# A two-layer graph network on one core: layer 1's weighted sums computed with features on partitions and turned back

## The chip, the cores and the metric

The kernel runs on one core of one Trainium2 chip. The metric is device time in microseconds (us) of one execution, the median of several runs. TensorE (PE) multiplies matrices, VectorE (DVE), ScalarE (ACT) and GpSimd (POOL) work elementwise, and SyncE (SP) issues DMA transfers. Each engine works through its own instructions in program order; between engines only semaphores order the work.

## The reference

There are 16 graphs of 1024 nodes with 256 features each, in float32. Cut to what matters (`_layernorm`, weights and `SCALE` are as one expects):

```python
# layer 0: attention with 8 heads of 32 features over the neighbours
h = jnp.maximum(_layernorm(x), 0.0)
Q, K, V = proj(Wq, bq), proj(Wk, bk), proj(Wv, bv)
scores = jnp.where(adj[:, None] == 0, -inf, einsum('bhnd,bhmd->bhnm', Q, K) * SCALE)
out = einsum('bhnm,bhmd->bhnd', softmax(scores), V)
x = x + einsum('bno,po->bnp', merge_heads(out), Wo) + bo
# layer 1: scores between nodes, a softmax, and a weighted sum of h
h = jnp.maximum(_layernorm(x), 0.0)
e_k = leaky_relu(einsum('bid,bjd->bij', h * a_k[:, 0], h), 0.2)   # k = 0..3
scores = -9e15;  scores = e_k where adj == k + 1
x = x + einsum('bij,bjd->bid', softmax(scores), h)                # <- the sums
```

adj holds only 0 and 1 here, so the kernel computes layer 1 with a_0 alone and has a branch for other kinds that is not taken.

## The kernel before, in words

A tile is 128 nodes (rows) of one graph, so there are 16 x 8 = 128 tiles (`NT` = 8 per graph). One long pipeline runs over steps `s` = 0 to 128; `t` is `s` modulo 8. In one step the kernel does, side by side: attention of tile `s` (`now`), the end of attention of tile `s` - 1 (`was`), layer 1's scores and softmax of tile `s` - 9 (`edge`), the weighted sums and the output of tile `s` - 10 (`edge_was`), and the projections of tiles 8 and 9 ahead (`piece_was`, `piece`). After the last step a short loop over `tiles` (lines 987 to 1012) finishes the last nine layer-1 tiles; it is called the tail below.

The order of work is written by hand (`tc.manual_schedule()`): the order of the code is the order of the instructions on each engine. A step is a loop over eight heads `h`, and each `h` has a fixed order: `now.scores(h)` on PE (line 461, one tile of 128x1024 scores in PSUM), `now.softmax_max(h)` on DVE (line 473, adds the mask and takes the row's maximum), `softmax_exp` of the head before on ACT (line 490), then the turning of the head before that, either by PE transposes (line 590) and a copy (line 591) or by DVE's block transposition (`blocks_of`, line 381) and DMAs (`placed`, line 386), and then the extra work of that `h`. For the tile with t = 7 heads 4 and 5 are turned by PE, for t = 0 heads 0 and 1; for all others heads 0, 1, 4 and 5 go by blocks.

Scores are in two PSUM tiles, `sides`. Once layer 1 runs, heads 4 and 6 use `sides[1]` and all others `sides[0]`, so that scores(1), for example, can't start before softmax_max(0) has read `sides[0]`. Layer 1's scores (line 633, and transposes of mirrored blocks in line 627) use `sides[1]` in h = 0 to 2.

The other small results on PSUM live in two banks of 2 x 256 columns: `sums_place` and `brief` in the first, `early` and `late` in the second:

```python
sums_place, brief, early, late = (banks[i // 2][:, i % 2, :] for i in range(4))
```

What bears on the change, in a step's order. h = 4: `output` (PE, line 541, into `late`), `raised(1)` (ACT, line 309, reads `early`). h = 5: `residual` (DVE, line 547, reads `late`), layer-norm statistics (DVE), `gather(0)` (PE, line 698), `piece.turn` (PE, two transposes, line 237, into `late`), `turned` (ACT, lines 249 and 250). h = 6: scores(6), `gather(1)`, softmax_max(6), `store` (DVE, lines 705 and 707, and the output's DMA on SP, line 708), blocks of head 4, `project(0, ...)` (PE, line 267, eight instructions, into `late`). h = 7: scores(7), softmax_max(7), blocks of head 5, `combine(0)` (PE, line 526, writes `sums_place`), `raised(0)` (ACT, line 309, reads `late`).

`gather` computes the sums for one layer-1 tile. The transposed weights `pT` have 128 source nodes on partitions; `h1s` holds the normed features. For each of the eight blocks `j` of source nodes and each group `a` of 32 target nodes a matmul takes 32 columns of `pT` as the stationary operand and all 256 features as the moving one; its output goes to 32 partitions, so that four matmuls (`a` = 0 to 3) sit in four column groups of the array. A float32 matmul is two instructions in the trace; so there are 32 matmuls or 64 instructions for a tile. Target nodes are on partitions in the result, as the output wants them.

In the tail two PSUM places alternate for the sums: `sums_place` for even tiles, `late` for odd ones.

Of the kernel before, what the change touches and what calls it, by code (L numbers as in the profile page):

```python
# [14 lines left out]
ALU = mybir.AluOpType  # L15
AX = mybir.AxisListType

P = 128
HEADS = 8
HD = 32  # L20
# [22 lines left out]
def by_chunk(place):  # L43
    return place.rearrange("p (c n) -> p c n", n=P)
# [3 lines left out]
def gnn_kernel(  # L48
# [18 lines left out]
    nc = tc.nc  # L67
    B, N, D = x.shape
    NT = N // P
    NC = D // P  # L70
    SCALE = HD ** (-0.5)
    HALF = 512
    NB = P // HD
# [21 lines left out]
    sums_place, brief, early, late = (banks[i // 2][:, i % 2, :] for i in range(4))  # L95
# [5 lines left out]
    ident = const.tile([P, P], F32, name="ident")  # L101
# [269 lines left out]
    def mixed(rows):  # L371

        return rows.rearrange("(b k) n -> k b n", b=NB)
# [18 lines left out]
    h1s, x1ds, masks = {}, {}, {}  # L392
# [201 lines left out]
    class Edges:  # L594
# [98 lines left out]

        def gather(self, half):

            for j in range(half * NT // 2, (half + 1) * NT // 2):
                for a in range(NB):
                    nc.tensor.matmul(  # L698
                        self.sums[a * HD : (a + 1) * HD, :], lhsT=self.pT[:, j, a], rhs=h1s[self.b][:, j, :],
                        start=(j == 0), stop=(j == NT - 1),  # L700
                    )

        def store(self):
            rec = small.tile([P, 1], F32, tag="rec1")
            nc.vector.reciprocal(rec, self.total)
            ot = self.buffer("h0", [P, D])
            nc.vector.scalar_tensor_tensor(ot, self.sums, rec, self.x1, ALU.mult, ALU.add)  # L707
            nc.sync.dma_start(out=mixed(out[self.b, self.rows, :]), in_=ot)


    def layer_1_of_kinds(b):
# [75 lines left out]
    with tc.manual_schedule():  # L787
# [51 lines left out]
        for s in range(B * NT + 1):  # L839
            b, t = divmod(s, NT)  # L840

            def load_keys(h, end):
                if t == NT - 1 and b + 1 < B and 2 * h + end in KEY_STEPS:
                    load_key(b + 1, KEY_STEPS.index(2 * h + end))
                if t == 0 and 0 < b < B and 2 * (HEADS + h) + end in KEY_STEPS:
                    load_key(b, KEY_STEPS.index(2 * (HEADS + h) + end))

            nxt2, edge_nxt, piece_nxt = attend_of(s + 2), edges_of(s + 1), piece_of(s + 1)
            for h in range(HEADS):
                ending, eh = (now, h - 1) if h >= 1 else (was, HEADS - 1)  # L850
                turning, th = (now, h - 2) if h >= 2 else (was, HEADS + h - 2)

                load_keys(h, 0)


                if now:
                    now.scores(h)
                if h == 0 and piece_was:
                    piece_was.halve(0)
                if s == 0 and h == 1:  # L860
                    first[1].values()
                if h == 3 and edge:
                    edge.softmax_max()
                if h == 5:
                    if was:
                        was.residual()
                    norms(was, piece_nxt)
                if h == 6 and edge_was:
                    edge_was.gather(1)
                if now:  # L870
                    now.softmax_max(h)
                if h == 6 and edge_was:
                    edge_was.store()


                if h == 1 and edge:
                    edge.keep(0)
                if h == 2 and gone:
                    gone.turned_normed()
                if ending:  # L880
                    ending.softmax_exp(eh)

                if h == 3 and was:
                    was.turned_reciprocals()
                if h == 3 and edge:
                    edge.bend()
                    edge.keep(1)


                if h == 3:  # L890
                    if was:
                        was.combine(1)
                    if piece_was:
                        piece_was.biased()
                    if was:
                        was.combined()
                if turning and th in by_blocks(turning.t):
                    turning.turn_blocks(th)
                    turning.place_blocks(th)
                elif turning:  # L900
                    turning.turn(th, 0)
                    turning.turn(th, 1)


                if h == 0:
                    if edge:
                        edge.score(0)
                    if gone:
                        gone.normed()
                    if edge_was:  # L910
                        edge_was.turn_blocks()
                        edge_was.place_blocks()
                if h == 1:
                    if gone:
                        gone.turn_normed()
                    if piece_was:
                        piece_was.project(1, 0)
                        piece_was.project(1, 1)
                    if was:
                        was.reciprocals()  # L920
                    if piece_nxt:
                        piece_nxt.load()
                if h == 2:
                    if edge:
                        edge.score(1)
                    if piece_was:
                        piece_was.values()
                    if was:
                        was.turn_reciprocals()
                        was.add_bias()  # L930
                if h == 3:
                    if nxt:
                        nxt.load_queries()
                    if edge:
                        edge.leak()
                    if edge_was:
                        edge_was.load_nodes()
                    if nxt:
                        nxt.flag()
                        nxt.mask()  # L940
                if h == 4:
                    if was:
                        was.output()
                    if piece_was:
                        piece_was.raised(1)
                        piece_was.halve(1)
                    if piece:
                        piece.normed()
                    if piece_was:
                        piece_was.write_queries()  # L950
                    if edge_nxt:
                        edge_nxt.prepare()
                    if nxt2:
                        nxt2.load()
                if h == 5:
                    if edge_was:
                        edge_was.gather(0)
                    if piece:
                        piece.turn()
                    if piece:  # L960
                        piece.turned()
                if h == 6:
                    if edge:
                        edge.softmax_exp()
                    if was:
                        was.keep()
                    if now:
                        now.load_nodes()
                    if piece:
                        piece.project(0, 0)  # L970
                        piece.project(0, 1)
                if h == 7:
                    if now:
                        now.combine(0)
                    if piece:
                        piece.raised(0)
                load_keys(h, 1)
            gone, was, now, nxt = was, now, nxt, nxt2
            edge_was, edge = edge, edge_nxt
            piece_was, piece = piece, piece_nxt  # L980
# [7 lines left out]
        for i in range(1, len(tiles) + 2):  # L988
            edge = tiles[i] if i < len(tiles) else None
            if edge:  # L990
                edge.score(0)
                edge.score(1)
            if i <= len(tiles):
                tiles[i - 1].turn_blocks()
                tiles[i - 1].place_blocks()
            if i >= 3:
                tiles[i - 3].store()
            if i >= 2:
                tiles[i - 2].load_nodes()
            if edge:  # L1000
                edge.keep(0)
                edge.keep(1)
                edge.softmax_max()
                edge.bend()
                edge.leak()
                edge.softmax_exp()
            if i + 1 < len(tiles):
                tiles[i + 1].prepare()
            if i >= 2:
                tiles[i - 2].gather(0)  # L1010
                tiles[i - 2].gather(1)
        tiles[-1].store()


# [50 lines left out]
```

## Time and profile before

| | |
|---|---|
| median of 3 runs | 3076.24 us (3071.88 to 3076.31) |
| the profiled execution | 3076.4 us, of which the span from first to last instruction is 3074.5 us |
| mean granted TensorE clock | 0.996 |
| PE busy | 2965.6 us (96%) |
| ACT busy | 2654.5 us (86%) |
| DVE busy | 2515.6 us (82%) |
| POOL busy | 2177.6 us (71%) |

Busy time adds up the times at which at least one instruction of an engine is under way. PE's instructions overlap: a matmul of 128 columns lasts some 0.27 us in the trace, but the next one starts long before its end. What PE takes for something is therefore read from start to start in the timeline, not from the durations. In timeline lines, the first number is the start in us from the span's start, the second the time from the first start to the last end in the merged line, "x8" the number of instructions, and a bracket the idle time ahead and what ended it.

### The profile page before, as it was taken

The page shows a single profiled execution, that of the slowest core. Times are in us where ns is not written, and L with a number is a line of the kernel's source. Part 1 is how long each engine was busy: PE and PEld are TensorE (multiplying, and loading weights), DVE is VectorE, ACT ScalarE, POOL GpSimd, SP SyncE. Part 2 cuts the span into 40 slices and gives each one's busy share as a digit, 9 for nine tenths or more (in the row PEclk, how much of TensorE's full clock was granted, in tenths as well). Part 3 has the DMA queues.
Part 4 walks back from the last instruction along what each step waited for, and adds up shares of the span by engine and source line. Part 5 has one row for each costly group of instructions (what it writes and reads, how often), then busy time and mean ns, then how long its engine had stood idle before and what let it go on. Part 6 is the DMA issues. An engine that isn't in the chain of part 4 may idle for free. (4 is left out here: it accounts for less than half of the span.)

```text
span 3074.5 us, 96254 instructions
## 1 busy us (share of the span) xinstructions
PE 2965.6 (96%) x36722; PEld 2230.1 (73%) x36722; DVE 2515.6 (82%) x4453; ACT 2654.5 (86%) x5159; POOL 2177.6 (71%) x2999
## 2 busy tenths in 40 slices
PE   7889999999999999999999999999999999999998
PEld 5667777777777777777777777777777777776664
DVE  5878888888888888888888788888888888888885
ACT  5888888899898998889889888988989888898882
POOL 3657777777777777777777777777777777776542
PEclk9999999999999999999999999999999999999999
DMA  7766777877777786777777777787777777777653
GB/s 245 219 219 205 237 235 222 255 216 243 231 225 243 230 257 209 232 247 220 246 230 228 235 232 243 221 255 221 220 247 228 251 211 235 237 227 236 191 168 100
DMA packets 597828, 695.68 MB, mean 226 GB/s; under 512 B 63280, under 2 KB 528560, under 8 KB 597360
## 3 DMA queue, kind: packets, MB, share of 16 engines
q1 hardware_dynamic: 528288, 477.29, 51.9%
q0 software_dynamic: 66960, 210.04, 21.0%
q8 instruction: 295, 4.83, 0.7%
q10 hardware_dynamic: 2112, 2.10, 0.2%
q14 instruction: 173, 1.42, 0.1%
HBM read 252.98 MB, written 134.22 MB: 126 GB/s over the span
## 5 line engine op out<-in xcount | busy, mean ns | idle before, releaser
L473 DVE CUSTOM_DVE_ANT_0 p<-s,neg 128x1024 f32<-128x1024 f32 x1024 | 1236.2, 1208 | 220.7 <-PE s L461 185.1
L490 ACT ACTIVATE p<-p,nmx 128x1024 f32<-128x1024 f32 x1024 | 1249.4, 1224 | 132.5 <-DVE nmx L473 123.9
L461 PE MATMUL s<-k,qt 128*128 128x512 f32 x2048 | 760.6, 453 | 15.5 <-DVE nmx L473 4.3
L591 ACT COPY pT<-trp 128x512 f32<-128x512 f32 x1024 | 549.4, 590 | 95.3 <-PE trp L590 94.9
L590 PE MATMUL trp<-ident,p 128*128 128x128 f32 x4608 | 604.5, 274 | 4.7 <-ACT pT L591 1.5
L590 PEld LDWEIGHTS trp<-ident,p 128*128 128x128 f32 x4608 | 531.0, 140 | 104.0 <-ACT pT L591 10.8
L381 DVE STREAM_TRANSPOSE blocks<-p 128x1024 f32<-128x1024 f32 x456 | 564.5, 1238 | 12.3 <-ACT p L680 10.6
L526 PE MATMUL acc<-pT,v 128*32 128x128 f32 x16384 | 533.4, 275 | 41.8 <-ACT recT L520 30.0
L526 PEld LDWEIGHTS acc<-pT,v 128*32 128x32 f32 x16384 | 453.5, 110 | 153.0 <-ACT recT L520 85.0
L698 PE MATMUL acc<-h,pT 128*32 128x256 f32 x8192 | 496.9, 382 | 2.8 <-DVE h L707 1.7
L441 POOL TENSOR_SCALAR neg<-adj 128x1024 bf16<-128x1024 int32 x128 | 467.9, 3655 | 42.9 <-ACT neg L453 33.7
L461 PEld LDWEIGHTS s<-k,qt 128*128 128x128 f32 x2048 | 322.9, 191 | 106.3 <-issue 43.0
L698 PEld LDWEIGHTS acc<-h,pT 128*32 128x32 f32 x8192 | 241.8, 109 | 207.8 <-issue 65.6
L676 POOL TENSOR_TENSOR sel<-sel,less 128x1024 f32<-128x1024 f32 x120 | 286.8, 2390 | 68.9 <-ACT less L665 47.6
L633 PE MATMUL s<-h1T,ha 128*128 128x512 f32 (+2 forms) x744 | 272.8, 490 | 2.7 <-ACT h1T L569 1.6
L674 POOL TENSOR_SCALAR less<-top 128x1 f32<-128x1 f32 x120 | 31.9, 266 | 274.0 <-DVE top L656 273.9
L324 POOL DMA_DIRECT2D qd<-halves x240 | 177.5, 780 | 58.7 <-POOL halves L314 31.8
L490 ACT ACTIVATION_READ_ACCUMULATOR p<-p,nmx 128x1 f32 x1024 | 206.8, 202 | 0.0
L510 POOL COPY wide<-rec 128x256 f32<-128x256 f32 x128 | 53.8, 420 | 204.2 <-DVE rec L508 204.2
L330 POOL DMA_DIRECT2D kd<-halves x240 | 172.2, 766 | 35.5 <-POOL halves L314 35.4
L314 POOL TENSOR_TENSOR halves<-full,halves 128x256 fp32r<-128x256 f32 x240 | 176.8, 737 | 20.6
L633 PEld LDWEIGHTS s<-h1T,ha 128*128 128x128 f32 x744 | 126.7, 190 | 70.7 <-issue 45.0
(117 smaller groups left out, 4328.4 us busy)
## 6 DMA issues: line engine op xcount, KB each, us to landing
pT<-blocks SPq DMA_DIRECT2D x2304, 128.0 KB, 3.5
qt<-qd SPq DMA_DIRECT2D x128, 512.0 KB, 4.5
k<-kd SPq DMA_DIRECT2D x128, 512.0 KB, 7.3
adj<-in_adj POOLq DMA_DIRECT2D x127, 512.0 KB, 5.0
qd<-halves POOLq DMA_DIRECT2D x240, 256.0 KB, 2.7
kd<-halves POOLq DMA_DIRECT2D x240, 128.0 KB, 4.1
xb<-in_x POOLq DMA_DIRECT2D x128, 128.0 KB, 4.2
x1d<-x SPq DMA_DIRECT2D x128, 128.0 KB, 4.0
```

Source lines behind the costliest of these rows:

```text
L324: nc.gpsimd.dma_start(out=qds[self.b][self.first, oc].rearrange("p u w n -> p u (w n)"), in_=halves.unsqueeze(1).to_broadcast([P, 2, 2 * P]),)
L381: nc.vector.transpose(blocks.rearrange("p b j q -> p j b q"), p)
L441: nc.gpsimd.tensor_scalar(self.neg, self.adj, 0.0, MASKED, ALU.is_equal, ALU.mult)
L461: nc.tensor.matmul(self.ps[:, cols], lhsT=self.qt[:, h, :], rhs=keysets[self.b][h][:, cols], start=True, stop=True,)
L473: nc.vector.tensor_tensor_reduce(out=p, in0=sides[h in self.second], in1=self.neg, scale=-SCALE, scalar=FLOOR, op0=ALU.add, op1=ALU.min, a ...
L490: nc.scalar.activation(to, of, AF.Exp, bias=nmx, scale=-1.0, accum_out=self.sums[:, h : h + 1])
L526: nc.tensor.matmul(sums_place[r * HD : (r + 1) * HD, g * P : (g + 1) * P], lhsT=vs[self.b][:, j, place_of(h) : place_of(h) + HD], rhs=self ...
L590: nc.tensor.transpose(tr[:, j, :], p[:, jj * P : (jj + 1) * P], ident)
L591: copy(pT[:, half * 4 : half * 4 + 4, :], tr)
L633: nc.tensor.matmul(self.side[:, cols], lhsT=self.ha[:, c, :], rhs=h1T[:, c, cols], start=(c == 0), stop=(c == NC - 1),)
L676: nc.gpsimd.tensor_tensor(self.sel, self.sel, self.less, ALU.subtract)
L698: nc.tensor.matmul(self.sums[a * HD : (a + 1) * HD, :], lhsT=self.pT[:, j, a], rhs=h1s[self.b][:, j, :], start=(j == 0), stop=(j == NT - 1),)
```

## The change

The sums of a layer-1 tile are computed the other way round. `h1s` becomes the stationary operand: 128 source nodes by 128 features, a full set of 128 columns; the moving operand is `pT` with all 128 target nodes. There are 8 blocks x 2 halves of the features, 16 matmuls (32 instructions) of 128 columns each in place of 32 (64) of 256 columns in column groups. The result has features on partitions. DVE copies it from PSUM to SBUF (`gathered`), PE turns it back by two 128x128 transposes into `early` or `brief` (`turn_back`), and `store` reads that.

The places change too: both halves of `gather` stand in h = 5, ahead of `piece.turn` and of scores(6). `gathered` stands in h = 6 behind softmax_max(6), where `store` stood. `turn_back` is PE's first work in the last part of h = 6, ahead of `project(0, ...)`. `store` moves to h = 7, behind softmax_max(7), and writes its result into `x1` in place, from which the output DMA reads. The tail has `gathered` and `turn_back` straight ahead of each `store`.

```diff
         def gather(self, half):
-            for j in range(half * NT // 2, (half + 1) * NT // 2):
-                for a in range(NB):
-                    nc.tensor.matmul(
-                        self.sums[a * HD : (a + 1) * HD, :], lhsT=self.pT[:, j, a], rhs=h1s[self.b][:, j, :],
-                        start=(j == 0), stop=(j == NT - 1),
-                    )
+            cols = slice(half * P, (half + 1) * P)
+            for j in range(NT):
+                nc.tensor.matmul(
+                    self.sums[:, cols], lhsT=h1s[self.b][:, j, cols], rhs=self.pT[:, j],
+                    start=(j == 0), stop=(j == NT - 1),
+                )
+
+        def gathered(self):
+            self.gT = self.buffer("h0", [P, NC, P])
+            nc.vector.tensor_copy(self.gT, by_chunk(self.sums))
+
+        def turn_back(self):
+            self.back = brief if self.sums is late else early
+            for c in range(NC):
+                nc.tensor.transpose(by_chunk(self.back)[:, c, :], self.gT[:, c, :], ident)
 
         def store(self):
             rec = small.tile([P, 1], F32, tag="rec1")
             nc.vector.reciprocal(rec, self.total)
-            ot = self.buffer("h0", [P, D])
-            nc.vector.scalar_tensor_tensor(ot, self.sums, rec, self.x1, ALU.mult, ALU.add)
-            nc.sync.dma_start(out=mixed(out[self.b, self.rows, :]), in_=ot)
+            nc.vector.scalar_tensor_tensor(self.x1, self.back, rec, self.x1, ALU.mult, ALU.add)
+            nc.sync.dma_start(out=mixed(out[self.b, self.rows, :]), in_=self.x1)
...
-                if h == 6 and edge_was:
-                    edge_was.gather(1)
                 if now:
                     now.softmax_max(h)
                 if h == 6 and edge_was:
+                    edge_was.gathered()
+                if h == 7 and edge_was:
                     edge_was.store()
...
                 if h == 5:
                     if edge_was:
                         edge_was.gather(0)
+                        edge_was.gather(1)
...
                 if h == 6:
+                    if edge_was:
+                        edge_was.turn_back()
                     if edge:
                         edge.softmax_exp()
...
             if i >= 3:
+                tiles[i - 3].gathered()
+                tiles[i - 3].turn_back()
                 tiles[i - 3].store()
...
+        tiles[-1].gathered()
+        tiles[-1].turn_back()
         tiles[-1].store()
```

## Prediction

> **What bounds the kernel now.** I read the busy times first, then the groups, the waits, and the timeline of one middle step (t = 3) instruction by instruction, followed by the same stretch for other t.
>
> ```profile
> PE 2965.6 (96%) x36722; PEld 2230.1 (73%) x36722; DVE 2515.6 (82%) x4453; ACT 2654.5 (86%) x5159; POOL 2177.6 (71%) x2999
> ...
> L698 PE MATMUL acc<-h,pT 128*32 128x256 f32 x8192 | 496.9, 382 | 2.8 <-DVE h L707 1.7
> ```
>
> PE is busy nearly throughout. The waits agree: over the whole run PE's longest wait is small, while DVE waits for PE often, also for the last gather:
>
> ```profile
> DVE p L473 <- PE s L461: 185.1, 308, 1.8
> ...
> DVE h L707 <- PE acc L698: 80.9, 120, 2.7
> ...
> PE acc L526 <- ACT recT L520: 30.0, 43, 1.6
> ```
>
> So a step (22.1 us for t = 6 to 24.4 for t = 0, from scores(0) to scores(0)) is as long as what PE issues in it plus what PE must wait for. The timeline of the stretch that the change rewrites:
>
> ```profile
> 844.62 0.38 PE L565 MATMUL acc<-ident,h 128*128 128x128 f32 x2
> 844.84 1.06 PE L267 MATMUL acc<-hTm,wqT 128*128 128x128 f32 x8
> 845.65 0.71 PE L461 MATMUL s<-k,qt 128*128 128x512 f32 x2
> ...
> 854.50 1.03 PE L590 MATMUL trp<-ident,p 128*128 128x128 f32 x8
> 854.60 0.64 ACT L309 ACTIVATE full<-acc,bq_t 128x128 f32<-128x128 f32 x2
> ...
> 855.32 0.42 DVE L547 TENSOR_TENSOR x<-acc,xb 128x256 f32<-128x256 f32 x1 [0.68 <-issue]
> 855.46 1.93 PE L698 MATMUL acc<-h,pT 128*32 128x256 f32 x32
> ...
> 857.33 0.44 PE L237 MATMUL acc<-ident,h 128*128 128x128 f32 x2
> 857.52 0.71 PE L461 MATMUL s<-k,qt 128*128 128x512 f32 x2
> ...
> 858.17 1.93 PE L698 MATMUL acc<-h,pT 128*32 128x256 f32 x32
> 858.27 1.23 DVE L473 CUSTOM_DVE_ANT_0 p<-s,neg 128x1024 f32<-128x1024 f32 x1 [0.20 <-PE s L461]
> ...
> 859.42 0.09 DVE L473 DVE_READ_ACCUMULATOR2_ANT nmx<- 128x1 f32 x1
> ...
> 860.03 1.16 PE L267 MATMUL acc<-hT,wkT 128*128 128x128 f32 x8
> 860.23 0.48 DVE L707 SCALAR_TENSOR_TENSOR h<-acc,rec,x1b 128x256 f32<-128x256 f32 x1 [0.64 <-PE acc L698]
> 860.63 1.23 DVE L381 STREAM_TRANSPOSE blocks<-p 128x1024 f32<-128x1024 f32 x1
> 860.95 0.72 PE L461 MATMUL s<-k,qt 128*128 128x512 f32 x2
> 861.78 1.19 DVE L473 CUSTOM_DVE_ANT_0 p<-s,neg 128x1024 f32<-128x1024 f32 x1
> ```
>
> PE goes without a hole from L590 (head 3) through gather(0), the two transposes of `piece`, scores(6), gather(1) and project to scores(7). All later sums start from these starts.
>
> **Gather itself.** Before: each half takes 1.87 us to the next start (855.46 to 857.33; 858.17 to 860.03), though DVE and ACT have nothing to do with it. Around them lie small changeover costs: L590 takes 0.96 us here where eight transposes elsewhere take 0.87 (843.75 to 844.62), scores(6) 0.65 where others take 0.55 (845.65 to 846.20), project 0.92 where others take 0.81 (844.84 to 845.65). From gather(0), with the 0.09 lost ahead of it, to scores(7): 860.95 - 855.46 + 0.09 = 5.58 us.
> After: 32 instructions of 128 weight columns and 128 moving columns, float32, each with new weights. L267 is the same form: (1.06 - 0.275) / 7 = 0.112 us apart, 0.275 being one instruction's duration. 32 x 0.112 = 3.58. That pT is read in pieces of 32 columns costs nothing: L526 reads the same layout and goes at 0.108 per four. PE alone would need 3.58 + 0.22 (two transposes, 844.62 to 844.84) + 0.55 (scores) + 0.22 (turn_back) + 0.81 (project) = 5.38: a gain of 0.20 us a step.
> The Trainium skill's page "TensorE: Matmul & The Clock Gate" (Back-to-back issue gap) gives N / 2.4 + 2.5 ns, 56 ns for 128 columns, without a word on float32. The row has twice that. By the page the gather would be 1.79 us and the whole change about even; I take the row.
>
> **The new wait.** turn_back is next on PE behind scores(6), and needs gathered, which stands on DVE behind softmax_max(6), which needs scores(6). Counted from the start of scores(6): softmax_max(6) starts at 0.75 (857.52 to 858.27), the next DVE instruction 1.15 later (859.42), the copy of 128x256 out of PSUM takes 0.42 (L547 and L355 have that size, 0.42 each), the hand-over to PE 0.06 (nmx to the next scores in h = 0). turn_back starts at 2.38, not at 0.55: PE stands for 1.83 us. Then 0.27 for two transposes from standstill (L237 shows 0.19 for two, its first 0.06 slower) and 0.81 for project: scores(7) at 3.46. So from gather(0) to scores(7): 3.58 + 0.22 + 3.46 = 7.26 us, against 5.58: **+1.68 us**. Queued behind turn_back on PE are project(0), scores(7) and combine(0), so softmax_max(7) on DVE and raised(0) on ACT come later too; nobody can use the hole, since PE's order is fixed. Before, DVE waited for PE here (0.64 us); now PE waits for DVE.
> For t = 7 head 4 is turned by PE between scores(6) and turn_back, eight transposes, 0.87 to 0.93 us (in the timeline 1506.43 to 1507.36). They cover half of the hole: 7.26 against 1508.17 - 1501.86 + 0.09 = 6.40, +0.86.
>
> **DVE at the step's end.** The removed store and its wait at h = 6 free DVE at a place where it will wait for PE anyway: no gain. At h = 7 store comes between softmax_max(7) and the blocks of head 5. From the start of scores(7): softmax_max(7) at 0.75, +1.15, +0.58 (reciprocal and store: 0.16 and 0.40 with gaps), +1.15 (blocks, 860.63 to 861.78): free at 3.63. scores(0) of the next step starts at 2.53 (0.64 + 1.89 for combine(0)), and softmax_max(0) would start 0.85 after it, at 3.38. So DVE is 0.25 late. Where scores(1) starts 0.05 us behind the end of softmax_max(0), which the timeline shows for t = 4 to 7 and 0, PE is late by as much; for t = 0 the t = 7 step ahead leaves DVE 1 us idle, which covers it. For t = 1 to 3 scores(1) starts 0.2 to 0.6 later than it could and covers it too. Bounds 0 to 0.6 us a step.
>
> **ACT at the step's end.** raised(0) reads `late`, store reads `early`, in one PSUM bank. L547 in the lines above started 0.08 us after the end of L309 and long after its own input: two readers of a bank are kept apart, in code order. So raised(0) must wait for store, from 0.8 to 2.6 us behind scores(7)'s start, and exp(7) behind it on ACT starts 1.2 later. ACT waits 0.66 + 0.5 us in the next two microseconds of a usual step and again 0.5 at head 2, which takes this up, except for t = 1, where PE's scores of layer 1 (L633) start at the end of ACT's L569: about +0.35 there. The skill's page "PSUM — Partial Sum Buffer" (PSUM bank collisions) asks for that separation by bank, and so speaks against putting store beside raised(0); it gives no price.
>
> **At nothing.** The output DMA on SP moves from h = 6 to h = 7, ahead of head 5's block DMAs, which wait for later DVE work. x1's buffer is released by this DMA (2.8 us to land) and not by store; its next writer comes some 8 us later. If that cover went, recT and combine(1) would wait up to 2.8 us.
>
> **Tail.** One iteration of DVE there takes 5.7 us (blocks to blocks). Added: copy 0.42, way to PE and back with two transposes 0.5, less the reciprocal that fits into it, 0.2: 0.7 for each of eight, 0.9 at the end, 0.6 in step 128: 7 us, by the same rows 0 to 15.
>
> **The sum.** Layer 1's sums run in steps 10 to 127 (118, of which 15 with t = 7) and in the tail. 103 x 1.68 = 173; 15 x 0.86 = 13; DVE 60 steps (t = 4 to 7) x 0.25 = 15; ACT 15 x 0.35 = 5; tail 7. Together 213 us. The profiled execution took 3076.4 us (span 3074.5 and 1.9 around it), 0.2 from the median. 3076 + 213 = **3289 us**.
>
> **The rivals.**
> *The wait is covered* (faster): if gathered could run before scores(6) is done, only the gain of 0.20 us stays: 118 x 0.20 = 24, less the tail's 7: 3059. It decides once PE has 1.83 us of own work between scores(6) and turn_back, or DVE does the copy ahead of softmax_max(6). Against it: the order on both engines is the code's, and only t = 7 has 0.9 us there. The page's pace for the gather would end near here as well. 4 in 100.
> *Half of the hole is won back*: later PE waits shrink, because DVE and ACT are ahead after it: 3076 + 107 = 3183. Against it: PE's own waits in a usual step are below 0.5 us in all. 8 in 100.
> *More is late at the step's end*: DVE by 0.6 us in all steps with the bound above and ACT's delay reaching PE in the next step: 0.5 x 118 = 59 more, 3348. For it: ACT is 86% busy. Also the clock: the tail, with PE 83% busy, shows 0.98 granted, which over all would be some 50 us. 10 in 100.
> *The sum above*: 78 in 100; with copies and hand-overs of +-0.1 us a step (12 us), a gather at 0.107 to 0.115 a piece (-19 to +11) and the bounds of DVE's term (-15 to +25) it spans 3250 to 3325.
>
> **How the numbers follow.** The range takes the sum's own span and reaches some way to the slow rival and to the one that wins back: 3230 to 3340; below lie most of the two rivals on that side, above a part of the last. A measurement here tells 0.2%, some 6 us, from no change; only the covered wait ends below that or near it: faster 0.04, same 0.02, slower 0.94.
>
> **What would show it.** Right: in the groups L698 becomes 4096 instructions of 128x128; PE waits for the DVE copy some 1.8 us in nearly every step, 190 to 200 us in all; the wait of DVE for L698 is gone; steps last 24 to 25 us, those with t = 7 grow by half as much. Wrong: the wait is there and the steps don't grow (won back), the wait is missing (covered), or the 32 instructions take clearly other than 3.6 us.

## The result and the profile after

The changed kernel takes 3267.86 us (median; 3267.2 to 3268.73), the kernel before 3075.32 in the same comparison: a ratio of 1.0628, 95% interval 1.061 to 1.0647. It is slower, 21 us below the forecast of 3289 and inside the range. The profiled execution has a span of 3266.5 us, 192.0 more than before.

The page of the changed kernel: busy times, and two groups of instructions (line 710 is turn_back's transpose; after the bar: busy us, mean ns of one; then the idle time ahead and what ended it).

```profile
PE 2954.0 (90%) x32882; PEld 2472.2 (76%) x32882; DVE 2554.1 (78%) x4581; ACT 2638.1 (81%) x5159; POOL 2167.4 (66%) x2999
...
L698 PE MATMUL acc<-pT,h 128*128 128x128 f32 x4096 | 480.6, 276 | 4.0 <-DVE x1b L715 2.3 <-DVE x L715 1.7
...
L710 PE MATMUL acc<-ident,h 128*128 128x128 f32 x248 | 51.1, 288 | 196.0 <-DVE h L705 194.4 <-DVE rec L714 1.6
```

PE has 3840 instructions fewer and about the same busy time, but its share of the span falls from 96 to 90%: it stands. Where, the waits of PE in steps 10 to 124 say (258 to 3110 us; us in total, times, longest):

```profile
PE acc L710 <- DVE h L705: 188.8, 115, 1.8
PE s L461 <- DVE nmx L473: 22.0, 64, 0.6
PE acc L526 <- ACT recT L520: 15.7, 31, 1.6
...
PE acc L526 <- DMA pT<-blocks: 1.1, 2, 0.9
```

The timeline of the same step as in the prediction (t = 3), from the gather on:

```profile
892.67 3.74 PE L698 MATMUL acc<-pT,h 128*128 128x128 f32 x32
...
896.24 0.38 PE L237 MATMUL acc<-ident,h 128*128 128x128 f32 x2
...
896.38 0.71 PE L461 MATMUL s<-k,qt 128*128 128x512 f32 x2
...
897.13 1.23 DVE L473 CUSTOM_DVE_ANT_0 p<-s,neg 128x1024 f32<-128x1024 f32 x1 [1.76 <-PE s L461]
...
898.27 0.42 DVE L705 COPY h<-acc 128x256 f32<-128x256 f32 x1
...
898.84 0.41 PE L710 MATMUL acc<-ident,h 128*128 128x128 f32 x2 [1.75 <-DVE h L705]
...
899.09 1.06 PE L267 MATMUL acc<-hT,wkT 128*128 128x128 f32 x8
...
899.90 0.70 PE L461 MATMUL s<-k,qt 128*128 128x512 f32 x2
...
900.64 1.22 DVE L473 CUSTOM_DVE_ANT_0 p<-s,neg 128x1024 f32<-128x1024 f32 x1 [0.79 <-PE s L461]
...
901.79 0.08 DVE L473 DVE_READ_ACCUMULATOR2_ANT nmx<- 128x1 f32 x1
901.79 0.16 DVE L714 RECIPROCAL rec<-total 128x1 f32<-128x1 f32 x1
902.04 0.48 DVE L715 SCALAR_TENSOR_TENSOR x1b<-acc,rec,x1b 128x256 f32<-128x256 f32 x1
...
902.44 1.23 DVE L381 STREAM_TRANSPOSE blocks<-p 128x1024 f32<-128x1024 f32 x1
```

From scores(6) (896.38) VectorE starts softmax_max(6) after 0.75 us, the copy after 1.89, and PE's turn_back after 2.46, where it could have stood at 0.55. Both engines wait for each other in turn: DVE 1.76 us for scores(6), while PE gathers, then PE 1.75 for DVE.

By the starts of scores(0), the steps grow as follows (medians over steps 16 to 119, us):

| t | 0 | 1 | 2 | 3 | 4 | 5 | 6 | 7 |
|---|---|---|---|---|---|---|---|---|
| before | 24.40 | 23.79 | 23.05 | 22.73 | 22.46 | 22.45 | 22.17 | 23.93 |
| after | 26.07 | 25.43 | 24.69 | 24.39 | 24.39 | 24.39 | 24.08 | 24.90 |
| more | 1.67 | 1.64 | 1.64 | 1.66 | 1.93 | 1.94 | 1.91 | 0.97 |

### The profile page after: what moved, and what is told of

It reads as the page before. It is cut to its first block, busy times and chain, and to the rows that moved or that the text cites. A ratio compares the mean times of both kernels' runs of the same rounds, so it can differ in the third digit from the quotient of the medians.

```text
span 3266.5 us, 88982 instructions
## 1 busy us (share of the span) xinstructions
PE 2954.0 (90%) x32882; PEld 2472.2 (76%) x32882; DVE 2554.1 (78%) x4581; ACT 2638.1 (81%) x5159; POOL 2167.4 (66%) x2999
## 5 line engine op out<-in xcount | busy, mean ns | idle before, releaser
L473 DVE CUSTOM_DVE_ANT_0 p<-s,neg 128x1024 f32<-128x1024 f32 x1024 | 1235.5, 1207 | 440.4 <-PE s L461 431.7
L590 PEld LDWEIGHTS trp<-ident,p 128*128 128x128 f32 x4608 | 533.0, 140 | 99.2 <-ACT pT L591 10.7
L381 DVE STREAM_TRANSPOSE blocks<-p 128x1024 f32<-128x1024 f32 x456 | 563.8, 1236 | 11.1 <-ACT p L680 10.6
L526 PE MATMUL acc<-pT,v 128*32 128x128 f32 x16384 | 526.7, 275 | 31.0 <-ACT recT L520 29.2
L698 PE MATMUL acc<-pT,h 128*128 128x128 f32 x4096 | 480.6, 276 | 4.0 <-DVE x1b L715 2.3
L698 PEld LDWEIGHTS acc<-pT,h 128*128 128x128 f32 x4096 | 469.2, 192 | 6.2 <-DVE x1b L715 3.3
L309 ACT ACTIVATE full<-acc,bk_t 128x128 f32<-128x128 f32 x240 | 75.4, 367 | 203.6 <-PE acc L526 157.6
L710 PE MATMUL acc<-ident,h 128*128 128x128 f32 x248 | 51.1, 288 | 196.0 <-DVE h L705 194.4
L710 PEld LDWEIGHTS acc<-ident,h 128*128 128x128 f32 x248 | 25.1, 141 | 243.9 <-ACT p L490 207.1
```

What stands on the lines that cost most here:

```text
L381: nc.vector.transpose(blocks.rearrange("p b j q -> p j b q"), p)
L473: nc.vector.tensor_tensor_reduce(out=p, in0=sides[h in self.second], in1=self.neg, scale=-SCALE, scalar=FLOOR, op0=ALU.add, op1=ALU.min, a ...
L526: nc.tensor.matmul(sums_place[r * HD : (r + 1) * HD, g * P : (g + 1) * P], lhsT=vs[self.b][:, j, place_of(h) : place_of(h) + HD], rhs=self ...
L590: nc.tensor.transpose(tr[:, j, :], p[:, jj * P : (jj + 1) * P], ident)
L698: nc.tensor.matmul(self.sums[:, cols], lhsT=h1s[self.b][:, j, cols], rhs=self.pT[:, j], start=(j == 0), stop=(j == NT - 1),)
```

## The experiments

All but one start from the changed kernel. They ran on several chips, on which the kernel before took 3068 to 3075 us; a ratio is to the kernel before on the same chip, and differences of a few us between runs say nothing. The theory: PE stands because the copy is queued behind softmax_max(6). The rivals: the wide form of the sums is dear, or the added work at the step's end is.

**Copy ahead of softmax_max(6).**

```diff
+                if h == 6 and edge_was:
+                    edge_was.gathered()
                 if now:
                     now.softmax_max(h)
-                if h == 6 and edge_was:
-                    edge_was.gathered()
```

> The changed kernel (3268 us) with DVE's copy of the sums (gathered) ahead of softmax_max(6) instead of behind it. If the time went into PE standing at turn_back for a copy that is queued behind softmax_max(6): PE's wait for the copy falls from some 194 us to under 20, scores(7) starts 1.58 us after scores(6) instead of 3.5, and 204 us come off; DVE then has 5.2 us of work between scores(6) and the next softmax_max(0) with less PE time beside it, and gives back some 67: 3131, between 3066 (nothing given back) and 3160. If the wide gather or the added work at the step's end took the time instead: above 3230.

Measured 3139.6 us, ratio to before 1.0224 (1.0207 to 1.0241). 128 us come off, so the place of one DVE instruction of 0.42 us held two thirds of the loss. PE's wait for the copy is nearly gone, but turn_back now waits for something else, in the waits of this kernel:

```profile
PE acc L710 <- ACT hTm L250: 25.8, 95, 0.3
...
PE acc L710 <- DVE h L705: 1.9, 4, 0.6
```

L250 is ACT reading `late`; turn_back writes `early`, the other half of the same bank. scores(7) starts 2.07 us behind scores(6) and not 1.58. Only a part of that is the bank's: in the step with t = 3 turn_back stands free at 869.83 (scores(6) at 869.28 and its 0.55), the copy ends at 870.05, L250 at 870.21, and turn_back starts at 870.26. So the copy alone would have held it for about half of this time, and the bank adds some 0.15 us. Most of the rest of the way back to 3076 goes to DVE, whose work from softmax_max(6) on now bounds the end of the step (PE waits 43.5 us for L473, 4.3 before), and to the tail (11.1 us from step 127 on).

**turn_back behind project(0).**

```diff
                 if h == 6:
-                    if edge_was:
-                        edge_was.turn_back()
...
                         piece.project(0, 1)
+                    if edge_was:
+                        edge_was.turn_back()
```

> The changed kernel with turn_back behind project(0) on PE: eight instructions, 0.81 us, now stand in the hole. If the hole is the cause, 0.81 us come off in each of 118 steps, 96 us, less 3 for DVE: 3175, and PE's wait for the copy falls by the same, to about 100 us. If the hole only shows a lateness that has another cause: within 15 us of 3268.

Measured 3173.5 us, ratio 1.0334 (1.0317 to 1.0351). 94 us come off: work put in the hole costs next to nothing. PE's wait for the copy fell to 38.8 us, further than to the 100 expected, in part because project(0) now waits too, for ACT's L250 (42.0 us, 16.1 before).

**The copy twice.**

```diff
-            nc.vector.tensor_copy(self.gT, by_chunk(self.sums))
+            for _ in range(2):
+                nc.vector.tensor_copy(self.gT, by_chunk(self.sums))
```

> The changed kernel (3268 us) with DVE's copy of the sums done twice. If PE stands for max(6) and the copy behind it, every added 0.35 to 0.42 us of DVE there lengthens each of 118 steps by as much, and the tail by 9 x 0.4: 45 to 53 us more, 3313 to 3321. If DVE's work there were partly hidden: less than 25 more.

Measured 3393.28 us, ratio 1.1052 (1.1026 to 1.1078): 125 us more, two and a half times what was expected. The expected part is there: of the steps with t = 0 to 3 the shorter ones are about 0.45 longer than in the changed kernel (those with t = 4 to 6 about 0.2; why less was not followed up). But 48 of the steps 10 to 126 are longer by a further 1.6 to 2.0 us, and the mean granted clock is 0.971 instead of 0.995. The windows of two neighbouring steps of this kernel (us; busy us of PE, PEld, DVE, ACT, POOL; then the granted clock, the DMAs' share and GB/s):

```profile
899.00:901.20 2.20, 0.01 (x1) 0.01 (x1) 2.12 (x5) 2.20 (x4) 2.20 (x5) 1.00 0.60 239
901.20:902.20 1.00, 0.98 (x9) 1.00 (x10) 1.00 (x1) 1.00 (x3) 0.83 (x3) 1.00 0.13 37
902.20:903.90 1.70, 1.70 (x21) 1.04 (x24) 0.65 (x2) 0.42 (x2) 1.45 (x4) 0.61 0.92 299
903.90:906.40 2.50, 2.50 (x57) 2.15 (x49) 2.32 (x5) 1.13 (x3) 0.39 (x1) 0.58 0.79 200
906.40:908.00 1.60, 1.60 (x16) 1.47 (x13) 0.73 (x1) 1.02 (x3) 1.26 (x2) 1.00 0.89 289
925.40:927.60 2.20, 0.04 (x1) 0.00 (x0) 2.09 (x5) 2.20 (x4) 2.20 (x5) 1.00 0.57 223
927.60:931.20 3.60, 3.55 (x76) 3.05 (x76) 2.70 (x5) 1.46 (x4) 2.34 (x6) 1.00 0.60 190
```

After a hole of 2.2 us the clock falls to half for 3.4 us in one step (0.50 in the window 902.56 to 905.97; the rows above take in a little more), and stays at 1.00 in the next, after the same hole. Such a stretch lies in each of the 48 long steps and in none of the others. The changed kernel's holes, at most 1.8 us, leave the clock at 1.00 from 260 to 3100 us.

**The wide gather with its halves apart**, in the old order.

```diff
+                if h == 6 and edge_was:
+                    edge_was.gather(1)
                 if now:
                     now.softmax_max(h)
...
                         edge_was.gather(0)
-                        edge_was.gather(1)
...
                 if h == 6:
-                    if edge_was:
-                        edge_was.turn_back()
...
                         piece.project(0, 1)
+                    if edge_was:
+                        edge_was.turn_back()
```

> The wide gather in the old order: its first half in h = 5, its second half behind scores(6), as the halves stood before; the copy behind softmax_max(6) and turn_back behind project(0). PE then has 1.8 us of gather and 0.8 of project between scores(6) and turn_back, and should not wait for the copy (under 10 us in all). If the form of the sums costs nothing and the order all: 24 us less than before on PE, 15 more for store in h = 7, 12 more in the tail: 3079. If the form is dear: above 3150.

Measured 3081.65 us, ratio 1.003 (1.0016 to 1.0044). With copy, turn_back and wide matmuls all in place, nearly the whole loss is gone: it is the order that costs, and not the form of the sums. The steps with t = 0 to 3 are 0.28 to 0.30 us shorter than before, those with t = 4 and 5 equal: there PE waits for softmax_max(0) (21.5 us for L473 in all, 4.3 before). Those with t = 6 are 0.16 and those with t = 7 0.84 longer; in some of the latter PE waits for a block DMA (17.7 us of such waits in the whole run, 11.4 before). From step 127 on it is 12.5 longer.

**The old gather, halves together** (from the kernel before).

```diff
-                if h == 6 and edge_was:
-                    edge_was.gather(1)
...
                         edge_was.gather(0)
+                        edge_was.gather(1)
```

> The kernel before with its old gather in column groups, but both halves in h = 5, ahead of scores(6): the change's place without its form. One pair of changeovers less on PE, 0.29 us a step or 34 us; but VectorE then has softmax_max(6), store, blocks, softmax_max(7), blocks in 5.9 us from the start of scores(6), against 4.7 that PE leaves for it, and gives back 0.6 to 1.2 us in the steps with t = 1 to 7: 3140, between 3110 and 3160. If the place matters only through the copy: 3042.

Measured 3160.33 us, ratio 1.0299 (1.0284 to 1.0314), at the upper bound. So the place alone, without any copy, costs 92 us. VectorE is one cause, as expected (20.9 us of PE's waits for L473, 4.3 before); project's wait for ACT's L250 is another (41.9 us, 16.1 before), which I had not counted: turned comes later, since piece.turn stands behind the whole gather. These two and combine's wait for store (10.6 us) make about 53 us; the rest was not followed up.

**store in h = 6**, by two ways (the comments name the run; each has one of the two insertions):

```diff
-                if h == 7 and edge_was:
-                    edge_was.store()
...
                 if h == 6:
                     if edge_was:
                         edge_was.turn_back()
+                        edge_was.store()          # store_h6: ahead of project(0)
...
                         piece.project(0, 1)
+                    if edge_was:
+                        edge_was.store()          # store_after_project
```

> The changed kernel with store in h = 6, behind turn_back and behind the blocks of head 4 on DVE, and not in h = 7. If store between softmax_max(7) and the blocks of head 5 makes softmax_max(0) late, the steps with t = 4 to 7 lose 0.28 us each (24.39 to 24.1 for t = 4 and 5), the steps with t = 1 to 3 nothing: 60 x 0.28 = 17 us, 3251. If something else makes those steps grow by 1.94 where others grow by 1.65: no change.

Measured 3592.03 us, ratio 1.1702 (1.1682 to 1.1721): a bad miss. Its waits of PE:

```profile
PE acc L710 <- DVE h L705: 196.0, 122, 1.8
PE acc L267 <- DVE x1b L715: 151.4, 109, 1.7
```

project(0) writes `late` and now waits for store, which reads `early` in the same bank and stands ahead of it in the code, behind the blocks of head 4 on DVE. Two holes in a row also bring the clock down (mean 0.946).

> The changed kernel (3268 us) with store at the end of h = 6, behind project(0) in the code, and not in h = 7. In the run before, store stood ahead of project(0); both touch one PSUM bank, and PE then waited 1.4 us more for VectorE in each step. Behind project(0) this wait can't arise, since project is done before DVE comes to store. If store between softmax_max(7) and the blocks of head 5 is what adds 0.28 us to the steps with t = 4 to 7, they fall to 24.1 (t = 4, 5) and 23.8 (t = 6), the others stay: 3251. If the bank was not the cause of the loss in the run before: far above 3268 again.

Measured 3249.44 us, ratio 1.0592 (1.0576 to 1.0607). The steps with t = 4 and 5 fall to 24.13 and 24.12, t = 6 to 23.81, t = 0 to 3 stay.

**store last in h = 7**, behind the blocks of head 5 and raised(0):

```diff
-                if h == 7 and edge_was:
-                    edge_was.store()
...
                         piece.raised(0)
+                    if edge_was:
+                        edge_was.store()
```

> The changed kernel with store as the last work of h = 7: behind the blocks of head 5 on DVE and behind raised(0) on ACT. DVE has the same work ahead of the next softmax_max(0), but ACT's raised(0) and exp(7) no longer wait for store. If DVE's load adds the 0.28 us to the steps with t = 4 to 7: no change, 3268, with 24.4 for t = 4. If ACT's wait does: 3251, with 24.1 for t = 4.

Measured 3267.79 us, ratio 1.0639 (1.0621 to 1.0657), all steps as in the changed kernel. So of the two causes named it is DVE's load ahead of softmax_max(0) that makes the 0.27 us; ACT's wait for store costs nothing.

**The tail.** Own buffer for the output rows, then also the other bank (the run with both came first):

```diff
-            nc.vector.scalar_tensor_tensor(self.x1, self.back, rec, self.x1, ALU.mult, ALU.add)
-            nc.sync.dma_start(out=mixed(out[self.b, self.rows, :]), in_=self.x1)
+            ot = self.buffer("h0", [P, D])
+            nc.vector.scalar_tensor_tensor(ot, self.back, rec, self.x1, ALU.mult, ALU.add)
+            nc.sync.dma_start(out=mixed(out[self.b, self.rows, :]), in_=ot)
...
-            self.back = brief if self.sums is late else early
+            self.back = brief if self.last and self.sums is not late else early
```

> The changed kernel with only the buffer of its own for the output rows, without the other bank in the tail. With both, 6 us came off the tail. If GpSimd's wait for the output's DMA and PE's wait for ha behind it made them: 3262 again, and GpSimd's wait for that DMA is gone. If the bank did: 3267, and PE still waits 0.6 us for store in each tail iteration.

> The changed kernel with a buffer of its own for the output rows (that of gT, free by then) in place of x1, and in the tail with the turned sums in the bank that the next gather doesn't write. The steps stay as they are. In the tail GpSimd no longer waits for the output's DMA (26 us in all) and PE no longer 0.6 us for store ahead of each gather: of the tail's 12.6 us more than before some 6 come off: 3262. If the tail grew by the longer chain on VectorE alone: no change.

Measured 3265.12 (ratio 1.0636, 1.0618 to 1.0654) and 3261.51 us (1.0631, 1.0615 to 1.0647). The ratios, each to the kernel before on the same chip, don't tell these from the 1.0628 of the changed kernel; the traces tell more. From scores(0) of step 127 to the end: 106.6 us before, 119.3 in the changed kernel, 115.8 with the buffer, 113.6 with the bank too. By one traced execution each, the buffer is worth 3.5 us and the bank 2.2; the versions that leave the tail's code as it is have 117.4 to 120.6 in this stretch, so the second is not sure by time alone. In the changed kernel's waits:

```profile
POOL x1b L686 <- DMA out<-x1b: 25.6, 3, 15.5
...
PE acc L698 <- DVE x1b L715: 2.3, 4, 0.6
...
PE s L633 <- POOL hT L613: 1.9, 1, 1.9
```

With the buffer the first and the last of these waits are gone, though GpSimd then waits nearly as long in all for store itself (25.0 us, longest 11.9; 21.3 and 11.2 before). With the bank too, PE's wait for store is gone. The 7.0 us that are left over 106.6 are near the 8 that the prediction had for the longer chain; no run takes them apart.

**A version that draws on most of this** (it ran before copy_twice, store_last and own_out): halves apart, the copy on ScalarE behind exp(5), turn_back and store behind project(0), the two changes of the tail. What the cut below leaves out is as in halves_apart and own_out_bank.

```diff
-            nc.vector.tensor_copy(self.gT, by_chunk(self.sums))
+            nc.scalar.copy(self.gT, by_chunk(self.sums))
...
                 if h == 6:
                     if edge_was:
-                        edge_was.turn_back()
+                        edge_was.gathered()
...
                         piece.project(0, 1)
+                    if edge_was:
+                        edge_was.turn_back()
+                        edge_was.store()
```

> The wide gather with its halves apart (second half behind scores(6)), the copy on ScalarE behind exp(5), turn_back and store behind project(0) in h = 6, a buffer of its own for the output rows and the other bank in the tail. PE then does 0.29 us less in each step, VectorE only has what it had before, and no wait is left for the copy: 118 x 0.29 = 34 us off, 2 more in the tail: 3044 with the kernel before at 3076. If ScalarE, 86% busy, can't take the copy (0.37 us and a wait): 3070 or more.

Measured 3051.8 us beside 3068.03 of the kernel before, ratio 0.9942 (0.9927 to 0.9956): faster than the kernel before by 0.6%, half of what was expected. The two profiled executions differ by 27 us; that of the kernel before, at 3076.4, is one of its slower ones. The profile has steps with t = 0 to 6 that are 0.27 to 0.30 shorter; those with t = 7 are not (24.00), and the part from step 127 on is 4 longer, where 2 were expected. In its timeline PE goes on without a hole, and the copy and store fall into gaps of ACT and DVE:

```profile
846.04 0.71 PE L461 MATMUL s<-k,qt 128*128 128x512 f32 x2
...
846.59 1.95 PE L698 MATMUL acc<-pT,h 128*128 128x128 f32 x16
...
848.37 1.06 PE L267 MATMUL acc<-hT,wkT 128*128 128x128 f32 x8
848.62 0.37 ACT L705 COPY h<-acc 128x256 f32<-128x256 f32 x1 [0.40 <-PE acc L698]
...
849.26 0.38 PE L710 MATMUL acc<-ident,h 128*128 128x128 f32 x2
...
849.40 0.71 PE L461 MATMUL s<-k,qt 128*128 128x512 f32 x2
849.74 0.48 DVE L716 SCALAR_TENSOR_TENSOR h<-acc,rec,x1b 128x256 f32<-128x256 f32 x1 [0.52 <-PE acc L710]
```

## Why the prediction was right, point by point

**The gather.** 3.58 us forecast for 32 instructions; 892.67 to 896.24 is 3.57. The row of L267 held. The Trainium skill's page "TensorE: Matmul & The Clock Gate" (Back-to-back issue gap) would have had half of it by the formula that the prediction took. That section gives the formula for a single matmul, and 81 ns where each matmul has its own weight load, as here: an estimate of 2.59 us, still too little. For float32 the measurement decides.

**The hole.** turn_back at 2.38 us behind scores(6) forecast, 2.46 measured; scores(7) at 3.46 forecast, 3.52 measured; +1.68 a step forecast, +1.64 to 1.67 measured for t = 0 to 3. scores(7) came 0.06 us later than forecast, and the two transposes of `piece` took 0.08 less (896.24 to 896.38), so a part of the close fit is luck. Moving the copy, filling the hole and lengthening it moved the time as the theory says.

**t = 7.** 0.86 and 0.25 for DVE forecast, 0.97 measured.

**DVE at the step's end.** 0.25 forecast for t = 4 to 7, 0.27 measured for t = 4 to 6 (the step less the 1.66 of the others); store_after_project took it away, store_last showed that it is DVE.

**ACT at the step's end.** That raised(0) waits for store came true (in a step with t = 1 it starts 2.75 us behind scores(7), 0.80 before); the 0.35 us for t = 1 did not. ACT waits 0.58 us ahead of L647 in this step, which I had overlooked, and that takes the lateness up: L647 starts 3.37 us into the step, and 3.36 before. 5 us too much. The page "PSUM — Partial Sum Buffer" (PSUM bank collisions) spoke against store beside raised(0). In the runs a shared bank cost nothing there, some 0.15 us a step at turn_back in copy_first, and 1.4 in store_h6 (151.4 us in 109 steps).

**The tail** was the term that was sized too small: 12.7 us from step 127 on, against 7 for the tail and 1 for that step. What was put at nothing, the release of x1's buffer by a DMA, has cover in the steps but not in the tail, where the DMA stands on SP behind the blocks' DMAs; and PE waits for store by the bank.

**What came off.** The sum by parts of the span: steps 0 to 9, which have no gather, -2.1 us (not explained); steps 10 to 119 +172.8, against 192 forecast (96 x 1.68 + 14 x 0.86 + 56 x 0.25 + 13 x 0.35); steps 120 to 126 +8.6, against 13, since there is no `piece` left and the cost is only 1.14 to 1.30 us; the rest +12.7. For steps 10 to 119 the medians by t make 184. The other 11 are mostly single steps of the kernel before in which PE waited for the block DMAs, 10.7 us in all, 1.1 after; that the later combine no longer meets these transfers is my reading. That is a small part of the rival in which PE's waits shrink. The misses of ACT's term and of steps 120 to 126 on the one side and of the tail on the other partly cancel; that too is luck. And the span of 3250 to 3325 was narrower than its own terms: their bounds add up to 3243 to 3337.

## What to carry to other kernels

When a result that PE needs back is copied by another engine, look at what stands ahead of the copy in that engine's queue and what stands behind the consumer in PE's: here a copy of 0.42 us made PE stand for 1.75, because it queued behind an operation that itself waited for PE. Keep enough independent work on PE between producer and consumer, and count the waits of a bank, not of its halves. The form of the matmuls was worth 0.3 us a step (the last version against the kernel before, t = 0 to 6) and the order 1.9 (the changed kernel against the last version, t = 0 to 3).

## What the runs showed of the hardware that I had not expected

A hole of 2.2 us on PE, after some 19 us in which it was busy throughout (879.60 to 898.40 in copy_twice), brings the granted clock down to half for 3.4 us in some steps, and not in others. Holes of up to 1.8 us never did so in the changed kernel, but the length of a hole alone doesn't decide: in halves_apart one wait of 1.61 us for a DMA, ended at 2583.48, was followed by a clock of 0.50 (2583.61 to 2587.00). So a longer wait can be paid for beyond its own length: copy_twice lost 125 us, though PE's wait for the copy grew by 58 (251.9 us against 194.4); its 48 stretches of 3.4 us at half the clock are worth some 80 us (48 x 1.7, an estimate). The page "TensorE: Matmul & The Clock Gate" (HAM oscillation, and What's actually happening) speaks of gaps over some 3.4 us and of windows that run freely; the free windows agree with the same hole having both outcomes, but 2.2 us were enough here.
